# A two-layer graph-attention kernel: query numbers of 16 groups by GpSimd gathers, W2's loads begun by ScalarE and its stores by SyncE

## The chip, the cores and the metric

The kernel runs on one core of one Trainium2 chip. The metric is the device time of one execution in microseconds (us), as the median of several runs. Engines: TensorE (PE; its weight loads are PEld), VectorE (DVE), ScalarE (ACT), GpSimd (POOL), SyncE (SP). SyncE, ScalarE and GpSimd can begin DMA transfers, each from its own in-order queue of instructions; "SPq", "ACTq" and "POOLq" in a profile are such beginnings.

## What is computed

Two layers of relational graph attention over 3125 nodes of 768 features and 53125 edges sorted by destination, with three relations; then a residual and a layer norm. One layer, cut to what matters:

```python
xr = jnp.einsum('nd,rdf->rnf', x, W)          # a row per node and relation
oi, oj = xr[etype, dst], xr[etype, src]
alpha = leaky_relu(oi @ q + oj @ k, 0.2)      # per edge and head: 4 heads, then 1
e = jnp.exp(alpha - segment_max(alpha, dst)[dst])
a = e / (segment_sum(e, dst)[dst] + 1e-16)
out = segment_sum(a * oj, dst) + b            # then elu after the first layer
```

An edge's query number `oi @ q` depends on its destination and relation alone, so per node there are 3 relations x 4 heads = 12 of them in the first layer.

## The kernel before

The nodes are cut into 25 groups of up to 128. A group's edges lie in 17 slots of 128 (14 in group 0), one edge per partition. There are three stages. The first multiplies every node by the three W1 matrices and stores the rows in a table in DRAM (`tab1`, named ftab in the profile). The second gathers a row for each edge, slot by slot, with GpSimd's indirect DMAs (`gather_rows`, L468), and sums them by destination on TensorE; it also makes the table for the second layer, of which the third stage gathers. Products of 32-bit numbers are three TensorE products of high and low parts each. The scores of the second stage read the query numbers from `pall`, one for each slot, edge and head, which the first stage fills.

The first stage is one written-out order. Each turn of `phase1`'s loop (L787 on) issues what the table `ev` holds for it, then one piece of the dense products: 18 matmuls 386 or 398 columns wide into one of two result banks (`banks`, po in the profile). A group has 6 pieces. ScalarE copies the result into one of six half rows (`d_row`, L581), which frees the bank, and SyncE stores it (L583). Every engine runs its own instructions in that order and waits only for the data and buffers that an instruction needs. The turn at which a step is issued is `when(turn, step, ...)`.

In the same loop a group's query numbers reach its edges. The last piece of a group also holds the 12 query numbers per node. VectorE splits them into three bf16 parts (`split3`, L207 to L212) and SyncE stores them in `q1_d`. Later SyncE loads the group's destinations over all partitions (`s_load1`, 544 KB, tile sT, L530) and the nodes' query numbers (`q_load1`, tile q, L540); VectorE turns the destinations into a 0/1 matrix (`a_q`, L680) and the relations into another (`a_oh`, L686); TensorE multiplies (`a_q2`, 17 matmuls of 36 columns, results pq); VectorE picks by relation and adds (`a_q3`, L708 and L711) into `pall`.

The second layer's W2 is prepared there too, in 18 pieces of 128 rows: `w_load` begins a load from GpSimd's queue (L745; two transfers for a piece of the last two of six), `w_split` two turns later casts on ScalarE (L752) and subtracts on VectorE (L753) into the single tile w2hl, and takes two weighted sums (L756). Of the first 12 pieces both parts are stored in DRAM (`w2_d`): by SyncE for the first four, by GpSimd for the rest (L759), and read back late in the stage (`second_weights`). GpSimd has nothing else in the loop besides these transfers.

Of the kernel before, what the change touches and what calls it, by code (L numbers as in the profile page):

```python
# [9 lines left out]
F32 = mybir.dt.float32  # L10
# [3 lines left out]
I32 = mybir.dt.int32  # L14
AF = mybir.ActivationFunctionType
ALU = mybir.AluOpType
# [5 lines left out]
P = 128  # L22
# [4 lines left out]
BIG = float(2**100)  # L27
# [35 lines left out]
def _index(ap):  # L63
    return bass.IndirectOffsetOnAxis(ap=ap, axis=0)
# [3 lines left out]
SL = 17  # L68
# [13 lines left out]
WHOLE = 2  # L82
# [27 lines left out]
def kernel(  # L110
# [21 lines left out]
    nc = tc.nc  # L132
    N, D = x.shape
    R = layers[0]["W"].shape[0]
    E = src.shape[0]
    NB = (N + P - 1) // P
    NP = NB * P
    DT = D // P
    HALF = D // 2
    l1, l2 = layers  # L140
    H1 = l1["H"]
# [5 lines left out]
    HW = RW // 2  # L147
    EARLY = 6
    GB = NB - 4
# [4 lines left out]
    V, S, G, T = nc.vector, nc.scalar, nc.gpsimd, Counted(nc.tensor)  # L154
    OOB = float(1 << 20)

    dram = ctx.enter_context(tc.tile_pool(name="fdram", bufs=1, space=DRAM))
# [6 lines left out]
    tab2 = dram.tile([NP * R, RW], F32, name="ftab2")  # L164
    xb_d = dram.tile([NP + P, D], F32, name="xb_d")
    q1_d = dram.tile([NP + P, H1 * R * 3], BF, name="q1_d")
    w2_d = dram.tile([R * DT * P, 2 * D], F32, name="w2_d")

    ident = keep.tile([P, P], F32, name="fident")
# [26 lines left out]
    pall = keep.tile([P, NB, SL, H1], F32, name="pall")  # L196
# [7 lines left out]
    def split3(to, q, work, shape):  # L204

        c = work.tile(shape, F32, name="c3", bufs=2)
        V.tensor_copy(to[0], q)  # L207
        V.tensor_sub(c, q, to[0])
        V.tensor_copy(to[1], c)
        c2 = work.tile(shape, F32, name="c3", bufs=2)  # L210
        V.tensor_sub(c2, c, to[1])
        V.tensor_copy(to[2], c2)  # L212
# [242 lines left out]
    def slots(b):  # L455
        return SL if b else SLF
# [85 lines left out]
    def feature_rows(t):  # L542

        if t < H1:
            return [(0, t * F1, P)]
        o = P - (F1 - P)
        return [(0, (2 * (t - H1)) * F1 + P, F1 - P), (o, (2 * (t - H1) + 1) * F1 + P, F1 - P)]
# [31 lines left out]
    def d_row(o, q, b, p, po):  # L579

        S.copy(o[:, :HW], po[:, :HW])  # L581
        to = tab1[b * P * R:(b + 1) * P * R, :].rearrange("(p r) f -> p r f", r=R)
        nc.sync.dma_start(to[:, p // 2, p % 2 * HW:(p % 2 + 1) * HW], o[:, :HW])  # L583
        if p == len(PIECES1) - 1:
            q1s = q.tile([P, H1 * R, 3], BF, name="q1s", bufs=2)
            split3([q1s[:, :, i] for i in range(3)], po[:, HW:HW + H1 * R], q, [P, H1 * R])
            nc.sync.dma_start(q1_d[b * P:(b + 1) * P, :], q1s.rearrange("p k s -> p (k s)"))

    def stretches(rows, at_, a, e):

        i = a
        while i < e:
            c = at_(i) % len(rows)
            k, c = rows[c]
            n = 1
            while i + n < e and rows[at_(i + n) % len(rows)][0] is k and rows[at_(i + n) % len(rows)][1] == c + n:
                n += 1
            yield i, i + n, k[:, c:c + n, :]
            i += n

    def phase1(pre, work, psum, left, due, more):
        st = a_st
# [13 lines left out]
        def a_index2(b):  # L616
            pT = st[b]["pi"]
            c = SL
            V.tensor_scalar(dl[:, b, :], pT[:, c:2 * c], 1.0 / BIG, n_all[:, b:b + 1], op0=ALU.mult,
                            op1=ALU.subtract)  # L620
            inv = work.tile([P, SL], F32, name="inv", bufs=2)
            V.tensor_scalar(inv, dl[:, b, :], float(P), OOB, op0=ALU.is_ge, op1=ALU.mult)
            V.tensor_add(ridx[:, b, :], pT[:, 0:SL], inv)
            if b in first_rows:
                V.tensor_scalar(rfirst[:, first_rows[b], :], ridx[:, b, :], NP * R - 1, None, op0=ALU.min)
            V.tensor_copy(rel[:, b, :], pT[:, 2 * c:3 * c])

        counts = work.tile([32, 32], F32, name="counts", bufs=1)
        V.memset(counts, 0.0)
# [52 lines left out]

        def a_oh(b):
            s = st[b]
            s["oh"] = work.tile([P, SL, R * 3], F32, name="oh", bufs=2)
            V.tensor_tensor(s["oh"], rel[:, b, :, None].to_broadcast([P, SL, R * 3]),  # L686
                            rel3.rearrange("p r s -> p (r s)")[:, None, :].to_broadcast([P, SL, R * 3]),
                            op=ALU.is_equal)
# [46 lines left out]
        w2 = {}  # L735
        kq2 = work.tile([P, 2, D], F32, name="kq2", bufs=1)

        def w_load(i):
            if i == 0:
                for s, name in ((0, "k"), (1, "q")):  # L740
                    nc.sync.dma_start(kq2[:, s, :], l2[name].rearrange("f h -> h f").to_broadcast([P, D]))
            r, t = divmod(i, DT)
            w2[i] = share[3][:, :D]
            for p, at, n in feature_rows(t):
                G.dma_start(w2[i][p:p + n], l2["W"][r, at:at + n, :])  # L745

        def w_split(i):
            w = w2.pop(i)
            r, t = divmod(i, DT)
            if r < WHOLE:  # L750
                hl = work.tile([P, 2, D], F32R, name="w2hl", bufs=1)
                S.copy(hl[:, 0, :], w)  # L752
                V.tensor_sub(hl[:, 1, :], w, hl[:, 0, :].bitcast(F32))  # L753
            for s in range(2):
                j = work.tile([P, D], BF, name="w2j", bufs=1)
                V.scalar_tensor_tensor(j, w, 1.0, kq2[:, s, :], op0=ALU.mult, op1=ALU.mult,  # L756
                                       accum_out=wkq2[:, t, (Q2 if s else K2)[r]:][:, 0:1])
            if r < WHOLE:
                (G if i >= 4 else nc.sync).dma_start(w2_d[i * P:(i + 1) * P, :].rearrange("p (s f) -> p s f", s=2), hl.bitcast(F32))  # L759

        def pad_rows():

# [7 lines left out]
        def when(n, f, *a):  # L770
            ev.setdefault(n, []).append((f, a))

        TAIL = 6 * (GB - 1)
        S0 = 10
        when(8, pad_rows)
        for b in range(NB):
            c = S0 + 5 * b
            when(c - 3 if b else S0 - 1, c_load, work, b)
            when(c - 2 if b else S0 - 1, a_load, pre, b)
            when(c + 1, a_index, b)  # L780
            when(c + 2, a_index2, b)
            when(c + 1, c_next, b)
            q = max(c + 1, 6 * b + 2)
            if b < GB:
                k = (q, q, q, q + 3, q + 3, q + 4, q + 5)
            else:
                q = max(c + 2, 6 * GB + 4 + 2 * (b - GB))  # L787
                e = 6 * NB - 5 + b - GB
                k = (q, 6 * NB - 14 + b - GB, 6 * NB - 5, q + 5, e, e, e)
            for n, f in zip(k, (s_load1, q_at, q_load1, a_q, a_oh, a_q2, a_q3)):  # L790
                when(n, f, b)
            if b > 1:
                t, e = {2: (2, 4), 3: (3, 10), GB: (TAIL - 8, TAIL - 3), GB + 1: (TAIL - 7, TAIL), GB + 2: (TAIL - 6, TAIL - 2), GB + 3: (TAIL - 5, TAIL - 1)}.get(
                    b, (6 * b - 11, 6 * b - 8))
                when(t, d_load, b)
                when(e, d_split, b)
            when(5 * b + 2, p_load, b)
            when(5 * b + 5, p_plus, b)
        when(S0 + 5 * NB, a_last)
        for i in range(R * DT):  # L800
            when(6 * (2 + i), w_load, i)
            when(6 * (2 + i) + 2, w_split, i)
        for p, (r, f, n) in enumerate(((0, 0, HW), (0, HW, D - HW), (1, 0, HW), (1, HW, D - HW))):
            when(TAIL + 4 * p + 5, second_weights, r, f, n)
        for c in range(2):
            when(TAIL + 10 + 8 * c, second_kq, c)
        for n in range(2, max(max(ev), 6 * NB) + 1):
            if n < 10:
                more(2)
            for f, a in ev.get(n, ()):  # L810
                f(*a)
            next(left, None)
            while len(due) > (n < 6 * NB - EARLY - 1):
                d_row(outs[len(outs_used) % len(outs)], work, *due.pop(0))
                outs_used.append(0)
# [715 lines left out]
    with tc.manual_schedule():  # L1531
        with tc.tile_pool(name="share", bufs=1) as pool:
# [5 lines left out]
            with tc.tile_pool(name="wbuf", bufs=1) as wbuf:  # L1538
                weights[0] = [wbuf.tile([P, DT, WA], F32R, name=f"wa{s}") for s in "HL"]
                with tc.tile_pool(name="wrest", bufs=1) as wrest, tc.tile_pool(name="pre", bufs=1) as pre:  # L1540
# [16 lines left out]
                    with tc.tile_pool(name="work0", bufs=1) as work, tc.tile_pool(  # L1557
                        name="psum0", bufs=1, space=PSUM
# [22 lines left out]
                    with tc.tile_pool(name="work1", bufs=1) as work, tc.tile_pool(  # L1581
                        name="psum1", bufs=1, space=PSUM
                    ) as psum:
                        pools.append(psum)
                        phase1(pre, work, psum, left, due, more)
                with tc.tile_pool(name="exbuf", bufs=1) as exbuf:
                    extra = exbuf.tile([P, NX, RW], F32, name="extra")
                    with tc.tile_pool(name="work2", bufs=1) as work, tc.tile_pool(
                        name="psum2", bufs=1, space=PSUM
                    ) as psum:  # L1590
                        phase2(work, psum)
                    with tc.tile_pool(name="work3", bufs=1) as work, tc.tile_pool(
                        name="psum3", bufs=1, space=PSUM
# [545 lines left out]
```

## Time and profile before

| | us |
|---|---|
| runs | 1765.5, 1759.7, 1765.43; median 1765.43 |
| profiled execution | 1765.7 |
| its span | 1763.9 |
| last dense product of the first stage starts at | 530.5 |
| first row gather of the second stage starts at | 534.3 |
| first matmul of the second stage starts at | 551.4 |

| engine | busy us of the span | instructions |
|---|---|---|
| TensorE | 1648.9 (93%) | 14093 |
| VectorE | 1116.9 (63%) | 3911 |
| ScalarE | 438.0 (25%) | 805 |
| GpSimd | 901.3 (51%) | 907 |

In rows of groups, "x16 | 12.8, 538 | 188.5 <-DVE" means 16 instructions, 12.8 us busy, 538 ns each in the mean, and 188.5 us in which the engine stood idle just before them, with what ended it. In a timeline a row gives start, duration, engine, line, operation, what is written from what, and in brackets the idle time before it. In a table by stretch, each engine has its busy time and its count of instructions, then come TensorE's granted clock, the mean busy share of the 16 DMA engines, and GB/s. In a list of waits stand the total, the number and the longest.

### The profile page before, as it was taken

The numbers are of one execution on the slowest core, as the hardware profiler recorded it, in microseconds if no ns is written. First come the engines' busy times: TensorE is split into PE (matmuls) and PEld (weight loads), VectorE is DVE, ScalarE is ACT, GpSimd is POOL, SyncE is SP. The second block draws the span as 40 slices with busy tenths as digits, with TensorE's granted clock in tenths as the row PEclk, the third lists the DMA queues.
The fourth block names the chain that finished last, engine by engine and source line by source line (L and its number), as shares of the span: only waits on it lengthen the run. The fifth ranks groups of instructions, "written<-read, shape, count | busy, mean of one in ns | idle before, by whom it ended". The sixth has DMA issues, their size and how long they took to land. (4 is left out here: it accounts for less than half of the span.)

```text
span 1763.9 us, 38699 instructions
## 1 busy us (share of the span) xinstructions
PE 1648.9 (93%) x14093; PEld 1282.5 (73%) x14093; DVE 1116.9 (63%) x3911; ACT 438.0 (25%) x805; POOL 901.3 (51%) x907
## 2 busy tenths in 40 slices
PE   8999999999993899999999999939999999999996
PEld 8999999999992688888888888825444444444443
DVE  7566667566525666666677777455666666666663
ACT  6222222211210122121221112212333333333331
POOL 4100000000006777777777777057777777777760
PEclk9999999999996899999999999969999999999998
DMA  8576766656577999999999999469999999999970
GB/s 271 177 243 218 217 224 231 199 171 209 187 266 266 322 350 359 354 349 348 347 345 347 342 349 343 131 218 317 340 339 335 341 336 334 337 337 341 340 274 20
DMA packets 169367, 501.55 MB, mean 284 GB/s; under 512 B 39890, under 2 KB 82489, under 8 KB 169166
## 3 DMA queue, kind: packets, MB, share of 16 engines
q0 software_dynamic: 70832, 343.91, 55.1%
q1 hardware_dynamic: 90104, 144.97, 24.8%
q10 hardware_dynamic: 8230, 10.10, 1.7%
q8 instruction: 113, 1.85, 0.4%
q14 instruction: 88, 0.72, 0.1%
HBM read 414.04 MB, written 89.63 MB: 286 GB/s over the span
## 5 line engine op out<-in xcount | busy, mean ns | idle before, releaser
L468 POOL DMA_INDIRECT extra<-ftab,ridx x296 | 301.6, 1019 | 94.4 <-issue 52.7
L53 PE MATMUL po<-waH,hT 128*128 128x386 f32 (+1 forms) x1200 | 326.2, 346 | 1.4 <-DVE hT L1031 0.7
L53 PE MATMUL po<-waH,xT 128*128 128x386 f32 x1104 | 294.6, 343 | 0.9 <-ACT xT L255 0.4
L468 POOL DMA_INDIRECT share<-ftab,ridx x209 | 211.5, 1012 | 68.9 <-issue 41.0
L53 PEld LDWEIGHTS po<-waH,hT 128*128 128x128 f32 x1200 | 216.6, 189 | 4.8 <-DVE hT L1031 1.1
L53 PE MATMUL D<-extra,AT 128*128 128x256 f32 (+1 forms) x600 | 211.4, 504 | 5.3 <-ACT AT L1399 5.3
L53 PEld LDWEIGHTS po<-waH,xT 128*128 128x128 f32 x1104 | 203.9, 190 | 1.4 <-DVE xT L256 0.8
L53 PE MATMUL po<-waL,hT 128*128 128x386 f32 (+1 forms) x600 | 203.0, 338 | 0.0
L53 PE MATMUL po<-waL,xT 128*128 128x386 f32 x552 | 188.3, 341 | 3.1 <-DVE wbH L416 3.0
L53 PEld LDWEIGHTS D<-extra,AT 128*128 128x128 f32 x600 | 113.9, 196 | 69.6 <-issue 48.3
L581 ACT COPY share<-po 128x386 f32<-128x386 f32 x150 | 72.3, 482 | 368.9 <-PE po L53 296.4
L53 PE MATMUL acc<-waL,marks 128*32 128x386 f32 (+1 forms) x860 | 151.9, 489 | 0.0
L53 PE MATMUL po<-wbH,xT 128*128 128x386 f32 (+1 forms) x552 | 147.5, 341 | 0.9 <-DVE g L410 0.9
L53 PE MATMUL acc<-waH,marks 128*32 128x384 f32 (+1 forms) x828 | 140.4, 493 | 0.7 <-DVE marks L1321 0.7
L53 PE MATMUL acc<-extra,marks 128*32 128x386 f32 (+1 forms) x564 | 129.5, 487 | 0.0
L468 POOL DMA_INDIRECT waL<-ftab,ridx x108 | 107.9, 999 | 33.6 <-issue 25.3
L53 PE MATMUL acc<-extra,sel 128*32 128x193 f32 x2736 | 122.9, 332 | 2.3 <-DVE sel L940 2.3
L468 POOL DMA_INDIRECT waH<-ftab,ridx x103 | 103.7, 1007 | 31.4 <-issue 25.3
L53 PEld LDWEIGHTS po<-waL,hT 128*128 128x128 f32 x600 | 113.3, 189 | 0.0
L53 PE MATMUL acc<-share,marks 128*32 128x384 f32 (+1 forms) x456 | 109.7, 487 | 0.0
L745 POOL DMA_DIRECT2D share<-in_L_gnn_W_dram x24 | 12.8, 538 | 188.5 <-DVE w2j L756 117.1
L53 PEld LDWEIGHTS acc<-extra,sel 128*32 128x32 f32 x2736 | 86.5, 111 | 30.4 <-issue 4.9
(286 smaller groups left out, 2990.9 us busy)
## 6 DMA issues: line engine op xcount, KB each, us to landing
ftab<-share SPq DMA_DIRECT2D x150, 193.0 KB
ftab<-r SPq DMA_DIRECT2D x50, 386.0 KB
sT<-dr_d SPq DMA_DIRECT2D x23, 544.0 KB
xb_d<-share SPq DMA_DIRECT2D x25, 384.0 KB
ftab<-y SPq DMA_DIRECT2D x100, 96.0 KB
share<-xb_d SPq DMA_DIRECT2D x25, 384.0 KB
share<-in_x_dram SPq DMA_DIRECT2D x24, 384.0 KB
out_dram<-share SPq DMA_DIRECT2D x24, 384.0 KB
```

Of the source, the lines that this page charges most:

```text
L53: return self.add(self.engine.matmul(to, weights, moving, **more), to, moving)
L468: return G.indirect_dma_start(out=to, out_offset=None, in_=tab, in_offset=_index(i[:, j:j + 1]), bounds_check=NP * R - 1, oob_is_err=False)
L581: S.copy(o[:, :HW], po[:, :HW])
L745: G.dma_start(w2[i][p:p + n], l2["W"][r, at:at + n, :])
```

## The change

`by_gather(b)` is true for groups 0 to 18 without 4, 9 and 14: 16 groups of 25. For these the steps `s_load1`, `q_at`, `q_load1`, `a_q`, `a_oh`, `a_q2` and `a_q3` are not issued any more. Instead every group's 12 query numbers per node are also copied as they are (`q1f`) and stored in a new table `q1r_d` with a row of four for each node and relation; `a_index2` makes the row number of each edge (`qi`), and `q_gather` has GpSimd gather a slot's rows straight into `pall`: 128 rows of 16 bytes, 269 times. `pall` is zeroed first, as rows out of bounds are not written. The tile `oh` has one buffer instead of two. All of W2's loads begin on ScalarE, and the stores of its first 12 pieces on SyncE, in a step of their own two turns after the split.

```diff
+    q1r_d = dram.tile([NP * R, H1], F32, name="q1r_d")
@@ d_row, a group's last piece
             nc.sync.dma_start(q1_d[b * P:(b + 1) * P, :], q1s.rearrange("p k s -> p (k s)"))
+            q1f = q.tile([P, R, H1], F32, name="q1f", bufs=2)
+            V.tensor_copy(q1f, po[:, HW:HW + H1 * R].rearrange("p (h r) -> p r h", h=H1))
+            nc.sync.dma_start(q1r_d[b * P * R:(b + 1) * P * R, :].rearrange("(p r) h -> p r h", r=R), q1f)
@@ a_index2
+            if by_gather(b):
+                d = work.tile([P, SL], F32, name="qd", bufs=2)
+                V.scalar_tensor_tensor(d, pT[:, c:2 * c], R / BIG, pT[:, 2 * c:3 * c], op0=ALU.mult, op1=ALU.add)
+                st[b]["qi"] = work.tile([P, SL], I32, name="qi", bufs=7)
+                V.tensor_add(st[b]["qi"], d, inv)
+        def by_gather(b):
+            return b < GB - 1 and b % 5 != 4
+        def q_gather(b, j):
+            n = (b + 1) * P * R
+            G.indirect_dma_start(out=pall[:, b, j, :], out_offset=None, in_=q1r_d[:n, :],
+                                 in_offset=_index(st[b]["qi"][:, j:j + 1]), bounds_check=n - 1, oob_is_err=False)
@@ a_oh
-            s["oh"] = work.tile([P, SL, R * 3], F32, name="oh", bufs=2)
+            s["oh"] = work.tile([P, SL, R * 3], F32, name="oh", bufs=1)
@@ w_load
-                G.dma_start(w2[i][p:p + n], l2["W"][r, at:at + n, :])
+                nc.scalar.dma_start(w2[i][p:p + n], l2["W"][r, at:at + n, :])
@@ w_split, w_store
-                (G if i >= 4 else nc.sync).dma_start(w2_d[i * P:(i + 1) * P, :].rearrange("p (s f) -> p s f", s=2), hl.bitcast(F32))
+                w2hl[i] = hl
+        def w_store(i):
+            nc.sync.dma_start(w2_d[i * P:(i + 1) * P, :].rearrange("p (s f) -> p s f", s=2), w2hl.pop(i).bitcast(F32))
@@ the table of turns
+        when(8, G.memset, pall, 0.0)
-            for n, f in zip(k, (s_load1, q_at, q_load1, a_q, a_oh, a_q2, a_q3)):
-                when(n, f, b)
+            if by_gather(b):
+                for j in range(slots(b)):
+                    when(max(6 * b + 9, c + 3) + j * 7 // SL, q_gather, b, j)
+            else:
+                for n, f in zip(k, (s_load1, q_at, q_load1, a_q, a_oh, a_q2, a_q3)):
+                    when(n, f, b)
             when(6 * (2 + i) + 2, w_split, i)
+            if i < WHOLE * DT:
+                when(6 * (2 + i) + 4, w_store, i)
```

On GpSimd, from the last transfers of the edge preparation on, the order before was this, with `share` the tile that W2's pieces are loaded into and `w_d` the table for its parts:

```order
L299 DMA share<-ed_d 125x553
L279 DMA ed_d<-e 125x425
L279 DMA dr_d<-share 125x425
L279 DMA ed_d<-e 125x425
L745 DMA share<-in_L_gnn_W_dram 128x768 x4
L745 DMA share<-in_L_gnn_W_dram 64x768 x2
L759 DMA w_d<-w2hl 128x1536
L745 DMA share<-in_L_gnn_W_dram 64x768 x2
L759 DMA w_d<-w2hl 128x1536
```

From the same place the order now is this, up to the second stage's first row gathers (ftab_62 is `tab1`):

```order
L300 DMA share<-ed_d 125x553
L280 DMA ed_d<-e 125x425
L280 DMA dr_d<-share 125x425
L280 DMA ed_d<-e 125x425
L842 MEMSET pall 128x1700
L644 DMA pall<-q1r_d,qi 128x4 x269
L469 DMA share<-ftab_62,rfirst 128x772 x9
```

W2's transfers have left GpSimd's queue, and the zeroing and 269 query gathers stand ahead of the row gathers.

On ScalarE, in the early loop of the first stage, the copies that free the result banks (po) stood before between the casts of x (xT) and of W2 (w2hl):

```order
L581 COPY share<-po_778 128x386
L581 COPY share<-po_777 128x386
L752 CAST w2hl<-share 128x768
L581 COPY share<-po_778 128x386
L581 COPY share<-po_777 128x386
L255 CAST xT<-xr 128x768
```

The same piece of a group now:

```order
L582 COPY share<-po_779 128x386
L582 COPY share<-po_778 128x386
L764 DMA share<-in_L_gnn_W_dram 128x768
L582 COPY share<-po_779 128x386
L582 COPY share<-po_778 128x386
L771 CAST w2hl<-share 128x768
L582 COPY share<-po_779 128x386
L582 COPY share<-po_778 128x386
L256 CAST xT<-xr 128x768
```

The load of a W2 piece stands in ScalarE's own queue now, two copies ahead of the cast that needs it.

More of the change, by code (lines that the diff above doesn't have):

```diff
@@ L758, in w_split @@
             if r < WHOLE:
-                (G if i >= 4 else nc.sync).dma_start(w2_d[i * P:(i + 1) * P, :].rearrange("p (s f) -> p s f", s=2), hl.bitcast(F32))
+                w2hl[i] = hl
+        w2hl = {}
+        def w_store(i):
+            nc.sync.dma_start(w2_d[i * P:(i + 1) * P, :].rearrange("p (s f) -> p s f", s=2), w2hl.pop(i).bitcast(F32))
         def pad_rows():
```

## The prediction

> **What bounds the kernel now.** I read the span first, then a table of busy time by stretch over the first stage, then who waited for whom on TensorE there, then the timelines of five engines where that stage ends.
>
> ```profile
> span 1763.9 us, 38699 instructions
> ...
> core 0: us, PE busy (x) PEld busy (x) DVE busy (x) ACT busy (x) POOL busy (x), PEclk, DMA share, GB/s
> ...
> 194.00:213.00 19.00, 19.00 (x123) 18.84 (x122) 14.07 (x59) 4.36 (x8) 1.12 (x2) 1.00 0.79 250
> ...
> 498.00:517.00 19.00, 19.00 (x109) 19.00 (x108) 2.49 (x6) 2.90 (x6) 0.00 (x0) 1.00 0.97 358
> ...
> PE po L53 <- DVE wbH L416: 3.0, 1, 3.0
> ```
>
> In the two stretches TensorE is busy for all of their 19 us at full clock, with VectorE, ScalarE and GpSimd partly or almost wholly idle. The last row is TensorE's longest wait between 45 and 530 us, 3.0 us in the weight preparation, before the groups' loop; the others add little over 1 us and lie there too. So the first stage lasts as long as TensorE's own list of matmuls.
>
> ```profile
> 530.49 0.34 PE L53 MATMUL po<-wbH,xT 128*128 128x398 f32 x1
> ...
> 530.91 0.48 ACT L581 COPY share<-po 128x386 f32<-128x386 f32 x1 [2.78 <-PE po L53]
> ...
> 531.41 0.32 SPq L583 DMA_DIRECT2D ftab<-share  x1
> ...
> 531.42 0.18 DVE L207 CAST q1s<-po 128x12 bf16<-128x12 f32 x1 [2.24 <-ACT share L581]
> ...
> 532.26 0.18 DVE L212 CAST q1s<-c 128x12 bf16<-128x12 f32 x1
> ...
> 534.34 1.12 POOL L468 DMA_INDIRECT share<-ftab,rfirst  x1 [113.32 <-DMA q_d<-q1s]
> ...
> 544.92 1.00 POOL L468 DMA_INDIRECT share<-ftab,rfirst  x1 [0.30 <-issue]
> ...
> 548.83 1.00 POOL L468 DMA_INDIRECT extra<-ftab,rfirst  x1 [0.30 <-issue]
> ...
> 550.73 0.22 DVE L881 TENSOR_TENSOR a<-pall,share 128x36 f32<-128x36 f32 x1 [3.90 <-issue]
> ...
> 551.39 0.80 PE L56 MATMUL pa<-fident,al 128*32 128x128 f32 x3 [10.28 <-DVE al L883]
> ```
>
> Read it as a chain: last table product, its copy, its store (VectorE splits the query numbers meanwhile), then GpSimd's first row gather of the second stage, then eight more of them before VectorE's first add. It hangs on the last product. GpSimd had been idle for 113 us before, so whatever ends the products earlier moves the whole second stage earlier, as long as GpSimd is free by then.
>
> **The change, part by part.** TensorE first: 16 of the 25 groups lose their 17 query matmuls, 272 in all.
>
> ```profile
> 107.48 0.34 PE L53 MATMUL po<-waH,xT 128*128 128x386 f32 x1
> 107.66 0.59 PE L53 MATMUL pq<-q,sT 128*128 128x36 bf16 x17
> 108.10 0.42 PE L53 MATMUL po<-waH,xT 128*128 128x386 f32 x1
> 108.36 0.34 PE L53 MATMUL po<-waL,xT 128*128 128x386 f32 x1
> ...
> 203.66 0.48 ACT L581 COPY share<-po 128x386 f32<-128x386 f32 x1 [1.96 <-PE po L53]
> 206.85 0.48 ACT L581 COPY share<-po 128x386 f32<-128x386 f32 x1 [2.71 <-PE po L53]
> ...
> 210.55 0.48 ACT L581 COPY share<-po 128x386 f32<-128x386 f32 x1 [2.48 <-issue]
> ```
>
> From the product before the block to the second product after it pass 108.36 - 107.48 = 0.88 us; two products alone take 2 x 3.19/18 = 0.35 us (3.19 = 206.85 - 203.66, a turn of 18 products). The block costs 0.53 us. ScalarE's copies give 3.70 - 3.19 = 0.51. I take 0.53, which is read on the engine itself: 16 x 0.53 = 8.5 us (8.2 by the other), all of it on the path.
>
> GpSimd gets 269 gathers of four numbers per partition (14 for group 0, 17 for 15 more). None of that kind is in the trace; the nearest have the same 128 indices and longer rows.
>
> ```profile
> L468 POOL DMA_INDIRECT extra<-ftab,ridx x224 | 229.7, 1025 | 72.4 <-issue 36.0 <-PE po L53 13.1 <-PE acc L53 11.2
> ...
> 551.00:1110.00 559.00, 539.19 (x6404) 460.53 (x6408) 386.24 (x1092) 106.69 (x232) 417.65 (x410) 0.98 0.96 340
> ...
> 571.00 1.37 POOL L468 DMA_INDIRECT share<-ftab,rfirst  x1 [0.30 <-DVE F L898]
> ...
> 92.94 1.71 DVE L613 STREAM_TRANSPOSE pi<-T 32x32 f32<-32x32 f32 x8 [1.98 <-DMA T<-ed_d]
> ```
>
> Lower end: 1.02 us each with no gap, 274 us. Upper end: every one as slow as 1.37 and 0.30 between, 1.67 us each, 449 us. I take the mean of 1.02 and the 0.30 gap: 1.32 us each, 355 us. The first may start near 95 us, once group 0's indices are turned (92.94 + 1.71), and GpSimd must be free at 534.34 - 8.5 = 525.8. That leaves 431 us for 269 gathers, 1.60 us each. So 1.32 is hidden with some 75 us to spare, spread over the stage as the groups come; 1.67 would end at 544, 18 us late. What makes 1.32 the nearer end is that 224 gathers average 1.02 in a stage in which VectorE is busy for 386 of 559 us, as much as in the first.
>
> The gathers' bytes, and what goes:
>
> ```profile
> 532.00:533.00 1.00, 0.00 (x0) 0.00 (x0) 0.59 (x4) 0.00 (x0) 0.00 (x0) 1.00 0.52 198
> 533.00:534.00 1.00, 0.00 (x0) 0.00 (x0) 0.00 (x0) 0.00 (x0) 0.00 (x0) 0.65 0.09 9
> ...
> 540.00:545.00 5.00, 0.67 (x17) 0.59 (x17) 4.62 (x11) 0.00 (x0) 3.78 (x5) 0.50 0.95 333
> ```
>
> In the second row all that moves is one store of query numbers, 128 pieces of 72 bytes: 0.09 us of the 16 DMA engines. A gather of 128 pieces of 16 bytes is nearest to that: 269 x 0.09 = 24 us over 430. The first row is one 193 KB store in 0.52 us, so the 16 broadcasts of 544 KB that go free 16 x 1.5 = 23 us. The two cancel. The other end is a gather of whole table rows (third row: 0.95 of 5 us for about 3.8 of them, 1.24 us each): 334 us, and the DMA engines would be full. Those carry 386 KB against 2 KB, so I do not take it.
>
> ScalarE gets 24 W2 load issues and, in its queue, what stands behind them: the copies that free TensorE's two result banks, and the cast of W2 (L752), which now waits for a load issued only two copies earlier.
>
> ```profile
> 183.71 0.42 SPq L250 DMA_DIRECT2D xr<-in_x_t_dram  x1
> ...
> 189.65 0.83 ACT L255 CAST xT<-xr 128x768 fp32r<-128x768 f32 x1 [1.99 <-DMA xr<-in_x_t_dram]
> ...
> 194.05 0.48 ACT L581 COPY share<-po 128x386 f32<-128x386 f32 x1 [3.19 <-PE po L53]
> ...
> 200.49 0.48 ACT L581 COPY share<-po 128x386 f32<-128x386 f32 x1 [2.71 <-PE po L53]
> 200.87 0.83 ACT L752 CAST w2hl<-share 128x768 fp32r<-128x768 f32 x1
> ```
>
> The load would be issued after the copy at 194.05, near 194.5, and is wanted at 200.9: 6.4 us. The slowest load of that size that ScalarE waited for in the loop took 183.71 to 189.65, 5.9 us. If it is late, the next copy, which would start at 203.66, may wait until its bank is wanted a turn later, at 206.8: it must start by 206.3, the 0.83 us cast before it by 205.4, and 10.9 us are allowed. I cost it at nothing. The bounds are nothing and, were every load 1 us later than that, 12 casts x 1 = 12 us. An issue like the first row's takes 0.42 us, against idle gaps of 2.7.
>
> SyncE loses 16 broadcasts and 16 query loads with their address reads, and gets 25 small stores and 8 more stores of W2's halves. It issues a row store within 0.5 us of its copy (530.91 to 531.41), and six half-row buffers stand behind that, so one issue of 0.32 us more or less costs nothing; a W2 store waits for a split of two turns before and has four turns, 12.8 us, until the next cast takes its tile. VectorE loses an equality, an outer test, two products and a sum for each of 16 groups; it gets two operations on 17 numbers for each, and 25 copies of 12 numbers from a result bank. Those copies hold the bank of a group's last piece longer, after five conversions (531.42 to 532.44, the product over at 530.83): released 1.8 us after the product, needed after 3.2. Cost nothing; 25 x 0.18 = 5 us if no slack were there. GpSimd's zeroing of the query numbers comes once, in its empty stretch before 95 us. One buffer less for the test's tile changes nothing, since VectorE writes and reads both in order.
>
> The sum is 1765.7 (the profiled execution, 1.8 over its span) - 8.5 = **1757.2 us**. The median of the runs shown, 1765.43, is the same to 0.3; one run of the three was 1759.7. A difference under 0.5% (8.8 us) is about what a measurement of this kernel cannot tell from no change, and the sum stands just inside it.
>
> **The rivals.** *GpSimd becomes the bound of the first stage* (slower). Place: its last query gather against its first row gather. It decides from 1.60 us a gather on. VectorE's long operations could hold GpSimd up:
>
> ```profile
> L756 DVE SCALAR_TENSOR_TENSOR w2j<-share,kq 128x768 bf16<-128x768 f32 x36 | 34.4, 955 | 1.8 <-DMA kq<-in_L_gnn_q_dram 0.9 <-DMA kq<-in_L_gnn_k_dram 0.3
> L732 DVE TENSOR_TENSOR share<-share 128x768 f32<-128x768 f32 x25 | 23.7, 950 | 17.0 <-DMA share<-in_x_dram 16.9
> ...
> L680 DVE TENSOR_SCALAR sT<-sT,cols 128x2176 bf16<-128x2176 bf16 x23 | 17.8, 776 | 1.0 <-DMA sT<-dr_d 1.0
> ...
> L753 DVE TENSOR_TENSOR w2hl<-share,w2hl 128x768 fp32r<-128x768 f32 x12 | 11.5, 956 | 10.8 <-ACT w2hl L752 10.8
> L256 DVE TENSOR_TENSOR xT<-share,xT 128x768 fp32r<-128x768 f32 x11 | 10.5, 954 | 14.2 <-ACT xT L255 14.2
> L256 DVE TENSOR_TENSOR xT<-xr,xT 128x768 fp32r<-128x768 f32 x10 | 9.6, 957 | 16.0 <-ACT xT L255 16.0
> ```
>
> These are 107.5 of 470 us (60 to 530), 23%. If GpSimd stood still in all of them, a gather would take 1.32/0.77 = 1.71 us, the last would end at 95 + 460 = 555, 29 us after 525.8, and the time would be 1757 + 29 = 1786. Against it: in the second stage VectorE is busier still and gathers take 1.02 against 1.00 with it idle (548.83). But the operations there are other ones, so I leave 9%.
>
> The Trainium skill has a rule for this: "SBUF — State Buffer", section "SBUF: two separate sides", says that VectorE and GpSimd share one pair of ports as an exclusive lock, taken by VectorE's fast modes and its operations on two SBUF inputs, and that DMA descriptors written by GpSimd starve meanwhile. By that rule the time is this rival's, 1786; the second stage's 1.02 us does not bear out a large loss, and no row of before shows a gather beside the operations listed.
>
> *The queues give the gain back* (about no change). ScalarE stands behind a W2 load or behind a transfer slot, the copies come late, TensorE waits for a bank: 12 casts x 0.7 us would return 8.4 us, time 1766. That needs loads of 10.9 + 0.7 = 11.6 us on average; for it speaks that ScalarE did wait for a load once it was 5.9 us old, against it that none was near 10. 11%.
>
> *The DMA engines fill up* because the small pieces cost like table rows: over 430 us they would carry the loop's own 0.79 x 430 = 340 us, less 23, and 334 more, 221 us too much: 1978. The bytes speak against it. 2%.
>
> **How the numbers follow.** Forecast 78%, with a range of its own of 1752 to 1761 (2 us for a side cost, 5.7 for the spread of the runs, mostly below). GpSimd 9%, queues 11%, DMA 2%. The range 1751 to 1769 takes in the forecast's and most of the queues' case and leaves out the 11% of the slower ones and a few per cent below. Faster by over 0.5% is below 1756.6: half of the forecast's case, 38%. Slower is GpSimd and DMA, 11%. The rest, 51%, is the same.
>
> **What would show it.** Right: 153 query matmuls, the last product near 522 us instead of 530.5, GpSimd's gathers at about 1.3 us and done before 470, the first row gather near 526, later stages as long as before. Wrong: TensorE waiting for ScalarE's copy near a W2 cast; query gathers still running when the last table store has landed; a DMA share near 1 all through the stage. It would also be wrong low if the stage's turns were shortened by more than the matmuls taken out, for which no row speaks.

## The result, and the profile after

The changed kernel took 1757.4 us (median of 16 runs, 1753.6 to 1762.0), the kernel before 1763.4 us beside it (16 runs, 1758.1 to 1768.2): ratio 0.9969, 95% interval 0.9957 to 0.9982, a gain of 5.5 us (3.2 to 7.6); the two medians lie 6.0 apart. The forecast was 1757.2, from a gain of 8.5. The median lies 0.2 us from it only because the three runs of before that it started from stood 2 us above the 16; the gain is the number to explain, and it was forecast too large.

The page of the profiled execution (1756.9 us), its span, the row of the new gathers (busy us and mean ns of one, then the idle time before them), and the answer for TensorE's query products (pq):

```profile
span 1755.2 us, 38591 instructions
...
L644 POOL DMA_INDIRECT pall<-q1r_d,qi x269 | 290.4, 1079 | 95.7 <-issue 77.7
...
L53 PE MATMUL pq<-q,sT x119: 177/178/211, 171.5 to 531.6; 128*128 128x36 bf16 x119
...
L53 PE MATMUL pq<-q,share x17: 190/194/195, 528.3 to 528.8; 128*128 128x36 bf16 x17
...
L53 PE MATMUL pq<-q,xr x12: 194/195/213, 531.9 to 532.3; 128*128 128x36 bf16 x12
...
L53 PE MATMUL pq<-q,w2j x5: 195/195/195, 532.3 to 532.4; 128*128 128x36 bf16 x5
...
L644 POOL DMA_INDIRECT pall<-q1r_d,qi x269: 992/997/1812, 97.4 to 468.4; - x135
```

These are 153 query products, as forecast. The same answer for before has 391, 17, 12 and 5; 272 are gone, as many as the 16 groups had. The last row is the gathers' shortest, median and longest time in ns, and when the first and the last started. One stretch of the loop, in the columns of the prediction's table, shows who got the work, TensorE as full as before and GpSimd busy for 15 of 19 us:

```profile
194.00:213.00 19.00, 19.00 (x109) 19.00 (x108) 10.06 (x40) 4.36 (x8) 15.03 (x14) 1.00 0.70 200
```

The end of the first stage, which answers to the prediction's second set of rows:

```profile
523.07 0.34 PE L53 MATMUL po<-wbH,xT 128*128 128x398 f32 x1
...
523.49 0.48 ACT L582 COPY share<-po 128x386 f32<-128x386 f32 x1 [2.78 <-PE po L53]
...
525.48 0.38 SPq L591 DMA_DIRECT2D q1r_d<-q1f  x1
526.82 1.00 POOL L469 DMA_INDIRECT share<-ftab,rfirst  x1 [57.40 <-DMA q1r_d<-q1f]
...
542.72 0.22 DVE L912 TENSOR_TENSOR a<-pall,share 128x36 f32<-128x36 f32 x1 [4.02 <-DMA share<-ftab,rfirst]
543.38 0.80 PE L56 MATMUL pa<-fident,al 128*32 128x128 f32 x3 [10.74 <-DMA extra<-ftab,rfirst]
```

The chain is as it was: last product, copy, first row gather 3.75 us after the product (3.85 before), nine gathers, second stage. It starts 7.4 us earlier, and GpSimd had been idle for 57.4 us when it was wanted. From the second stage's first matmul to the end of the span the two executions take the same, 1212.5 us before and 1211.8 after.

To tell the loop from the rest, two rows of ScalarE do: its 21st copy out of a result bank, just after the first group's query products in before, and its 150th, the last of the stage. Before, and then after:

```profile
107.90 0.48 ACT L581 COPY share<-po 128x386 f32<-128x386 f32 x1 [2.71 <-PE po L53]
```

```profile
107.91 0.48 ACT L582 COPY share<-po 128x386 f32<-128x386 f32 x1 [2.72 <-DMA ftab<-share]
```

With the last copies at 530.91 (a row of the prediction) and 523.49 the loop between takes 423.01 us before and 415.58 after: 7.43 less. Copy by copy, the difference grows by 0.45 to 0.53 us at each of the 16 groups and falls twice, by 0.70 at the copy near 182 us and by 0.47 near 453. At both places TensorE now waits for VectorE (waits of TensorE from 45 to 530 us; in before neither is there):

```profile
PE po L53 <- DVE fdl L623: 0.4, 1, 0.4
...
PE po L53 <- DVE q1f L590: 0.2, 1, 0.2
```

At both, TensorE goes on 0.15 us after the end of q1f's copy out of the bank; `fdl` is the operation of VectorE behind that copy.

### The profile page after: what moved, and what is told of

It reads as the page before. It is cut to its first block, busy times and chain, and to the rows that moved or that the text cites. A ratio compares the mean times of both kernels' runs of the same rounds, so it can differ in the third digit from the quotient of the medians.

```text
span 1755.2 us, 38591 instructions
## 1 busy us (share of the span) xinstructions
PE 1640.4 (93%) x13821; PEld 1274.8 (73%) x13821; DVE 1086.4 (62%) x3888; ACT 437.8 (25%) x805; POOL 1177.4 (67%) x1145
## 5 line engine op out<-in xcount | busy, mean ns | idle before, releaser
L644 POOL DMA_INDIRECT pall<-q1r_d,qi x269 | 290.4, 1079 | 95.7 <-issue 77.7
```

The source lines that it names most:

```text
L644: G.indirect_dma_start(out=pall[:, b, j, :], out_offset=None, in_=q1r_d[:n, :], in_offset=_index(st[b]["qi"][:, j:j + 1]), bounds_check=n ...
```

## The experiments

They ran on two kinds of chip. On one the kernel before takes 1762 to 1763 us; on the other, where eight of the twelve ran (four on each of two chips), 2001 to 2002 us. Each ratio is to the kernel before on the same chip. The table has the loop (21st to last copy) of each profiled execution, which can be compared across chips as long as TensorE alone sets it.

| kernel | before there, us | time, us | ratio (95%) | loop, us |
|---|---|---|---|---|
| before | 1763 | 1763.4 | | 423.0 |
| changed | 1763 | 1757.4 | 0.9969 (0.9957 to 0.9982) | 415.6 |
| r1, changed again | 1762 | 1757.8 | 0.9976 (0.9963 to 0.9989) | 415.6 |
| r2, gathers only | 1762 | 1805.9 | 1.0243 (1.0213 to 1.0274) | 460.3 |
| r3, bank copy first | 1762 | 1756.9 | 0.9971 (0.9957 to 0.9986) | 414.5 |
| e6, 18 groups, bank copy first | 1762 | 1758.2 | 0.9969 (0.9954 to 0.9985) | 413.4 |
| e1, queues only | 2001 | 2014.3 | 1.0068 (1.005 to 1.0085) | 423.1 |
| e3, without the gathers | 2001 | 2007.3 | 1.0026 (1.001 to 1.0042) | 415.5 |
| e2, gathers only | 2001 | 2172.8 | 1.0851 (1.0824 to 1.0877) | 584.4 |
| e4, bank copy first | 2001 | 2204.1 | 1.1037 (1.1002 to 1.1071) | 597.3 |
| e5, 20 groups | 2002 | 2237.9 | 1.1188 (1.1142 to 1.1235) | 635.7 |
| e10, W2's stores back | 2002 | 2182.4 | 1.0914 (1.0874 to 1.0954) | 582.4 |
| e8, two-input operations | 2002 | 2164.5 (one run) | | 564.9 |
| e9, one-input operations | 2002 | 2192.8 (one run) | | 594.7 |

**Queues only (e1).** `by_gather` is false for all groups; the new table, its copies and the zeroing are out.

```diff
-            return b < GB - 1 and b % 5 != 4
+            return False
```

> Only the queues are changed: W2's loads begin on ScalarE and its stores on SyncE; no group's query numbers are gathered, and the new table, its copies and the zeroing are not there. Theory (the gain is TensorE's lost query matmuls alone, the queues are worth nothing): 425 query matmuls stand again, the last dense product starts near 530.5 us, and the time is that of the kernel before, ratio 0.999 to 1.001. Rival A (the queues cost part of the gain, which is why 5.5 us were measured and not 8.5): 1 to 3 us slower than before, with TensorE waiting for ScalarE's copies near the loads. Rival B (the queues themselves bring the gain): 3 us or more faster.

The loop's first and last copy:

```profile
109.25 0.48 ACT L581 COPY share<-po 128x386 f32<-128x386 f32 x1 [2.71 <-PE po L53]
...
532.35 0.48 ACT L581 COPY share<-po 128x386 f32<-128x386 f32 x1 [2.78 <-PE po L53]
```

The loop is 423.1 us, that of before on the other chip to 0.1: in the first stage the move of the queues neither costs nor brings anything by itself. The whole time is 13.7 us over before's on that chip, against all three expectations. There is no trace of before from that chip, and where these lie stays open.

**Without the gathers (e3).**

```diff
-                    when(max(6 * b + 9, c + 3) + j * 7 // SL, q_gather, b, j)
+                    pass
```

> The changed kernel with the 269 query gathers left out, so that 16 groups' query numbers stay zero; indices, the new table, its copies and the queues stay. Theory (the gathers are hidden wholly): time as the changed kernel's, ratio to before 0.996 to 0.998, last product near 523.1 us. Rival (the gathers disturb VectorE or the transfers of the first stage, and that is the missing 1 to 3 us): 1 to 3 us faster than the changed kernel, last product at 520.5 to 522.3 us.

```profile
111.54 0.48 ACT L582 COPY share<-po 128x386 f32<-128x386 f32 x1 [2.72 <-PE po L53]
...
527.05 0.48 ACT L582 COPY share<-po 128x386 f32<-128x386 f32 x1 [2.78 <-PE po L53]
```

The loop is 415.5 us against 415.6 with them on the other chip, and TensorE has the same two new waits (0.4 and 0.2): the gathers cost TensorE nothing on the faster chip, so the microsecond between 8.5 and 7.4 is not theirs. Against e1 on the same chip the loop is 7.6 us shorter and the median 7.0 us.

**Bank copy first (e4, then r3 where before takes 1762 us).**

```diff
+            q1f = q.tile([P, R, H1], F32, name="q1f", bufs=2)
+            V.tensor_copy(q1f, po[:, HW:HW + H1 * R].rearrange("p (h r) -> p r h", h=H1))
             split3([q1s[:, :, i] for i in range(3)], po[:, HW:HW + H1 * R], q, [P, H1 * R])
...
-            q1f = q.tile([P, R, H1], F32, name="q1f", bufs=2)
-            V.tensor_copy(q1f, po[:, HW:HW + H1 * R].rearrange("p (h r) -> p r h", h=H1))
```

> The changed kernel with VectorE's copy of the query numbers out of the result bank (q1f) moved ahead of the five conversions of the split. Theory (part of the missing microsecond is TensorE waiting for that bank, 0.41 us at 449 us and 0.2 to 0.4 us near 179 us): the waits of TensorE on q1f go, what is left is behind ScalarE's copies and the split, the last product starts 0.3 to 0.9 us earlier than 523.1 us, and the time is 0.3 to 0.9 us lower, too little for the ratio to tell. Rival (the bank is held by the split anyway, whichever comes first): the same total of waits, now on the split's last operation, last product unchanged.

> The changed kernel with the copy q1f ahead of the split, once more. Where the kernel before takes about 1763 us: by theory the waits of TensorE on q1f go and the last product starts 0.3 to 0.9 us earlier than the changed kernel's 523.1; by the rival (the split holds the bank anyway) it stays within 0.2 us, with the same waits under another name; if the edit itself were what cost 10% on the other chip, it is at 1.10 here too. Where it takes about 2000 us: as the changed kernel beside it, to 1%.

r3's 21st and last copies:

```profile
105.20 0.48 ACT L582 COPY share<-po 128x386 f32<-128x386 f32 x1 [2.71 <-DMA ftab<-share]
...
519.71 0.48 ACT L582 COPY share<-po 128x386 f32<-128x386 f32 x1 [2.78 <-PE po L53]
```

Loop 414.51 us, 8.50 less than before: 16 x 0.53 = 8.5, the forecast's sum. Both of TensorE's new waits are gone, and with them 1.07 us. That is the term that the prediction had put at nothing. The ratio, as expected, can't tell it.

**The changed kernel again (r1).**

> The changed kernel once more, as it is. On the chip of the first four experiments the kernel before took 2001 us, not 1763, two kernels without gathers stood at 1.003 and 1.007 of it, and two with gathers at 1.085 and 1.104. Theory 1 (that chip, not the edits of those two kernels, makes the gathers dear): where the kernel before takes about 2000 us, the changed kernel is 8 to 10% slower too, ScalarE's copies start up to 20 us late while gathers run, and the last dense product starts near 720 us; where the kernel before takes about 1763 us, ratio 0.996 to 0.998 and 523 us. Theory 2 (those edits themselves cost that): the changed kernel is at 0.996 to 0.998 on either chip.

Ratio 0.9976 and a loop of 415.60 us, 0.02 from the first trace. Here r1 and r3 agree to 0.1% while on the other chip e4, the same file as r3, was 10% slower: the chip makes that, not the edit. That the changed kernel itself is slower there was not run; six kernels with its gathers were, and took 8 to 12% more than before.

**Gathers only (e2, then r2).** W2's loads and stores stand where they were before.

```diff
-                nc.scalar.dma_start(w2[i][p:p + n], l2["W"][r, at:at + n, :])
+                G.dma_start(w2[i][p:p + n], l2["W"][r, at:at + n, :])
...
-                w2hl[i] = hl
+                (G if i >= 4 else nc.sync).dma_start(w2_d[i * P:(i + 1) * P, :].rearrange("p (s f) -> p s f", s=2), hl.bitcast(F32))
...
-            if i < WHOLE * DT:
-                when(6 * (2 + i) + 4, w_store, i)
```

> Only the gathers are added: W2's loads and stores stand in the queues they had before, so that on GpSimd they stand behind query gathers. Theory (the move of the queues is a condition of the gain): a group's 17 gathers take 17 x 1.38 = 23.5 us against 19.15 us of a group's turns, so GpSimd falls up to some 14 us behind the order before a group without gathers lets it catch up; a W2 load then begins up to 14 us late where 5 us of slack were reckoned (10.9 allowed, 5.9 for the load), ScalarE's cast and the copies behind it are late, and TensorE waits some 9 us in all, perhaps 20: ratio to before 1.000 to 1.008, last product at 531 to 543 us. Rival (GpSimd's queue has room enough for both): as the whole change, ratio 0.996 to 0.998, last product near 523 us.

> The kernel with the gathers alone once more: W2's loads and stores stand in the queues they had before. Where the kernel before takes about 1763 us: by the theory that the move of the queues is a condition of the gain, GpSimd is up to 14 us behind its order when a W2 load stands in it, casts and copies come late, ratio 1.000 to 1.008, last product at 531 to 543 us; by the rival (GpSimd's queue has room for both) ratio 0.996 to 0.998, last product near 523 us. Where it takes about 2000 us: ratio near 1.085 as before.

ScalarE's waits for W2's loads from 90 to 575 us in r2 (total, number, longest), the beginning of a W2 load on GpSimd, and the cast that waited for it:

```profile
ACT w2hl L771 <- DMA share<-in_L_gnn_W_dram: 64.3, 9, 11.5
```

```profile
178.35 0.59 POOL L764 DMA_DIRECT2D share<-in_L_gnn_W_dram  x1
```

```profile
169.85 0.48 ACT L582 COPY share<-po 128x386 f32<-128x386 f32 x1 [2.71 <-PE po L53]
181.81 0.83 ACT L771 CAST w2hl<-share 128x768 fp32r<-128x768 f32 x1 [11.48 <-DMA share<-in_L_gnn_W_dram]
182.55 0.86 ACT L582 COPY share<-po 128x386 f32<-128x386 f32 x2
```

The load begins only after the gathers ahead of it, at 178.35; the cast, whose turn had come at 170.3, waits 11.5 us, and two copies behind it, starting at 182.55, run one right after the other, too late for TensorE. In the changed kernel no cast of W2 waits for its load. The direction was expected, the size not: 44.8 us more than the changed kernel's loop, against 9 to 20. Nine casts are late, not one. TensorE's waits of this stretch add up to 30.0 us, 26.6 of them for ScalarE's copies. The other 15 go with a lower granted clock, the third number from the end in r2's row for 109 to 200 us:

```profile
109.00:200.00 91.00, 77.05 (x426) 75.61 (x426) 45.98 (x189) 16.65 (x31) 66.29 (x64) 0.92 0.57 163
```

It is 0.95 to 0.97 from 200 to 500 us; the changed kernel has 1.00 in all of these. What lowers it is not shown.

**18 groups (e6).** With the bank copy first, as in r3.

```diff
-            return b < GB - 1 and b % 5 != 4
+            return b < GB - 1 and b % 10 != 9
```

> The changed kernel with 18 groups gathered instead of 16 (303 gathers; all but 9 of groups 0 to 18) and q1f ahead of the split. Theory (each group more takes 0.53 us from TensorE as long as GpSimd is done in time): at 1.38 us each the gathers end at 97 + 303 x 1.38 = 515 us, ahead of the 525 us at which the first row gather may start; last product near 521.5 us, time 1 to 2 us under the changed kernel's, ratio 0.995 to 0.997. Rival (GpSimd falls behind its order, since groups without a gather are what lets it catch up, and the last groups' gathers come after 525): first row gather up to 10 us later, ratio 1.000 to 1.004. Where the kernel before takes about 2000 us: worse than the changed kernel beside it, ratio over 1.10.

Its gathers, and its first row gather:

```profile
L644 POOL DMA_INDIRECT pall<-q1r_d,qi x303: 992/997/1778, 100.9 to 518.3; - x152
```

```profile
528.11 0.99 POOL L469 DMA_INDIRECT share<-ftab,rfirst  x1 [8.85 <-DMA q_d<-q1s]
```

Two groups more take 1.08 us more from the loop (413.43), against 2 x 0.53; 303 gathers take 417 us, 1.38 each, and end 8.85 us before GpSimd is wanted. This is about as many as fit, since another group's 17 take 23. The loop is the shortest of all, but the median is not below r3's or the changed kernel's. (The profiled execution, the slowest of its seven, reached its 21st copy at 111.39 us, 6.2 later than r3's; that tells nothing of the median.) A version measurably better than the changed kernel was not found.

**20 groups (e5) and W2's stores back (e10).**

```diff
-            return b < GB - 1 and b % 5 != 4
+            return b < GB - 1
```

```diff
-                w2hl[i] = hl
+                (G if i >= 4 else nc.sync).dma_start(w2_d[i * P:(i + 1) * P, :].rearrange("p (s f) -> p s f", s=2), hl.bitcast(F32))
...
-            if i < WHOLE * DT:
-                when(6 * (2 + i) + 4, w_store, i)
```

> The changed kernel with 20 groups gathered (0 to 19, 337 gathers) instead of 16. Theory (GpSimd becomes the bound when its gathers do not fit between 96 and 525 us, at 1.38 us each 310 of them): they end at 96 + 337 x 1.38 = 561 us; the last dense product comes 4 x 0.53 = 2.1 us earlier than the changed kernel's, the first row gather waits for GpSimd's own queue until 561 instead of 526, and the time is some 34 us over the changed kernel's: ratio to before 1.015 to 1.020. Rival (GpSimd keeps up, since its gathers shorten when VectorE has less to do for these groups): the gathers end before 525, ratio 0.994 to 0.997.

> The changed kernel with W2's stores back where they were, behind the split and for pieces 4 to 11 on GpSimd; its loads stay on ScalarE. Theory (only the loads had to leave GpSimd, since a cast waits for them): the stores stand behind gathers, their tile comes free late, but no load does; GpSimd waits some 10 to 20 us in all for the splits, its gathers end near 480 to 490 us, well before 525, and time and last product are the changed kernel's within 1 us, ratio 0.996 to 0.998. Rival (the stores cost too: the single tile w2hl is held until GpSimd has stored it, so the next cast on ScalarE and the copies behind it are late): TensorE waits for ScalarE's copies, 5 to 20 us, ratio 1.000 to 1.009.

Both ran on the slower chip, where the loop waits for something else, and neither answers its question: in e5 GpSimd stood idle for 69 us before its first row gather, so it was not the bound, and e10 lies between e2 and e4. Beyond 303 gathers the limit is untried, and so is which of loads and stores had to move.

What the slower chip does shows in e4's waits from 45 to 700 us, of TensorE, then of ScalarE, and in one of ScalarE's copies:

```profile
PE po L53 <- issue: 99.2, 17, 25.4
PE po L53 <- ACT share L582: 40.2, 7, 12.0
```

```profile
ACT share L582 <- remote: 232.4, 24, 29.0
```

```profile
168.66 0.48 ACT L582 COPY share<-po 128x386 f32<-128x386 f32 x1 [17.36 <-remote]
```

The product that this copy takes was done by 154.2, and the store that frees its half row, six copies earlier, was begun at 135.07, but it starts at 168.66, 2.3 us after the last of eleven gathers that ran meanwhile. Without gathers (e1, e3) the loop has none of this. What holds the copies there is not settled: "remote" says that the trace has no releaser, and no run tells the possible ones apart.

**Operations beside the gathers (e8, e9).** One more operation of VectorE in each of 90 turns, nothing reads its result.

```diff
+        def extra_op():
+            j = work.tile([P, D], BF, name="w2j", bufs=1)
+            V.tensor_tensor(j, kq2[:, 0, :], kq2[:, 1, :], op=ALU.add)   # e8
+            V.tensor_copy(j, kq2[:, 0, :])                               # e9, instead
...
+        for n in range(20, 110):
+            when(n, extra_op)
```

> The changed kernel with one more operation of VectorE in each of 90 turns of the first stage, 768 numbers per partition from two SBUF inputs (a sum of kq2's two halves into the scratch tile w2j, which nothing reads). In the changed kernel 47 of 269 gathers took over 1.1 us and lie beside such operations. Theory (VectorE's operations on two SBUF inputs hold GpSimd's gathers up): about as many more are stretched by about half a microsecond, the gathers' busy sum goes from 290 to 305 to 330 us and the last starts 15 to 40 us later than 468 us. Rival (it is a chance of the order; the gathers are stretched by something else): sum 288 to 293 us, end as before. By both TensorE's last product stays within 2 us.

> As the kernel beside it, but the operation added in each of 90 turns is a copy of 768 numbers per partition from one SBUF input. Theory (two SBUF inputs are what holds a gather up): the gathers' busy sum stays at 288 to 295 us and their end at 468 us to 5 us. Rival (any long operation of VectorE on SBUF does): the sum goes to 305 us or more, as with two inputs.

Both on a slower chip. Groups of e8, then of e9:

```profile
L644 POOL DMA_INDIRECT pall<-q1r_d,qi x269 | 304.0, 1130 | 187.7 <-issue 77.7 <-DVE qi L635 74.8 <-DMA q1r_d<-q1f 19.5
...
L787 DVE TENSOR_TENSOR w2j<-kq 128x768 bf16<-128x768 f32 x90 | 85.7, 952 | 0.8
```

```profile
L644 POOL DMA_INDIRECT pall<-q1r_d,qi x269 | 281.4, 1046 | 245.9 <-DVE qi L635 98.4 <-issue 77.4 <-DMA q1r_d<-q1f 32.4
...
L787 DVE CAST w2j<-kq 128x768 bf16<-128x768 f32 x90 | 51.3, 570 | 0.8
```

In e4, on another of the slower chips, with the bank copy first and without either operation, the sum is 279.8 us: 24 less than with the operations on two inputs, 2 less than with those on one. Read by the sums, two inputs would be what counts, as expected. The single gathers say otherwise. A copy of e9, and a gather that begins inside it:

```profile
361.97 0.56 DVE L787 CAST w2j<-kq 128x768 bf16<-128x768 f32 x1
```

```profile
362.10 1.30 POOL L644 DMA_INDIRECT pall<-q1r_d,qi  x1 [0.30 <-issue]
```

It finds 0.43 us of the copy left and takes 0.30 longer than 1.00. In e9, 29 gathers begin inside an added copy, and those with 0.16 to 0.43 us of it left take 0.03 to 0.30 longer: the rest less 0.13, which is also what an operation on two inputs costs. In e8, 38 begin inside an added sum and take 0.47 longer in the mean, 17.7 us in all. The copies cost only 2.0 in all because they are shorter (0.55 us against 0.95) and 11 of the 29 gathers meet one in its last 0.06 us. So one input from SBUF holds a gather up too, and the theory of e9 is wrong, though the sum hardly moved. When the gathers end can't be compared, since the loop itself is stretched.

## Why the prediction was right, and where not

**What bounds the kernel** and the chain at the stage's end were right: what came off the loop moved the second stage by as much or a little more (product 7.4 earlier, row gather 7.5, first matmul of the second stage 8.0).

**TensorE's 16 x 0.53 us** was right in the sum to 0.02 us: r3's 8.50 shows it, and e6 that two groups more give 2 x 0.54.

**"Cost nothing" for q1f's copy out of the bank** was the step that failed. It reckoned 1.8 us of holding against 3.2 of slack, from a place where VectorE came at once. At two places VectorE came late: near 178 us behind small operations of the edge preparation, near 448 behind one of 1.03 us and one of 0.95. The first of them, with TensorE's next product into that bank (the one before it had ended at 175.42):

```profile
178.00 0.17 DVE L209 TENSOR_TENSOR c<-po,q1s 128x12 f32<-128x12 f32 x1
...
178.71 0.16 DVE L590 COPY q1f<-po 128x12 f32<-128x12 f32 x1
```

```profile
179.02 0.41 PE L53 MATMUL po<-waH,xT 128*128 128x386 f32 x1 [0.40 <-DVE fdl L623]
```

Only the first two of the split's five conversions read the bank, the second of them at 178.00. So without q1f the bank is free 2.7 us after its product; with q1f behind all five it is held for 3.45 us, and for 3.80 at the other place. That cost 1.1 us, near the lower of the two ends given (0 and 5). r3 shows it by taking it away.

**From 7.4 to 5.5 us** (4.2, with 1.9 to 6.5, in r1) the rest is not shown. Most of both intervals lies below 7.4, so something outside the loop seems to take 2 to 3 us back. The two profiled executions do not show it: their spans differ by 8.7 us. Two things vary there between executions of one kernel: the start (21st copy at 107.91 and 106.01 in two traces of the changed kernel) and the granted clock, which in the loop of both kernels is 1.00. Over the runs of r1 and of before beside it the clock's mean was 0.9733 for before (22 runs) and 0.9721 for the changed kernel (10 runs); (1 - clock) x time is 47 and 49 us, 2 us of it. Among runs of equal clock (0.972, 0.973, 0.974) r1's lie 6.1, 5.8 and 6.3 us below before's, with 2 to 6 runs each. So the clock goes with a part of the difference; whether the change lowers it, and how, is not shown. Nor is it excluded that the move of the queues costs something outside the loop: e1's 13.7 us on the slower chip lie there.

**GpSimd's gathers.** Forecast 1.32 us each and done before 470; the pitch was 371.1/268 = 1.38, the last began at 468.4. They were hidden, with 57 us to spare. The 0.06 comes from 47 gathers of over 1.1 us, and they show how the rival (GpSimd becomes the bound) went wrong. VectorE and GpSimd of the changed kernel, in one place:

```profile
185.84 0.96 DVE L751 TENSOR_TENSOR share<-share 128x768 f32<-128x768 f32 x1 [3.11 <-DMA share<-in_x_dram]
187.65 0.96 DVE L257 TENSOR_TENSOR xT<-xr,xT 128x768 fp32r<-128x768 f32 x1 [0.85 <-ACT xT L256]
```

```profile
185.20 0.99 POOL L644 DMA_INDIRECT pall<-q1r_d,qi  x1 [0.30 <-issue]
186.50 1.17 POOL L644 DMA_INDIRECT pall<-q1r_d,qi  x1 [0.30 <-issue]
187.98 1.50 POOL L644 DMA_INDIRECT pall<-q1r_d,qi  x1 [0.32 <-issue]
```

The operation at 185.84 begins inside a gather, which stays at 0.99. The gather at 186.50 begins inside it, with 0.30 us of it left, and takes 0.17 longer; that at 187.98 finds 0.63 left of the next and takes 0.50 longer. So it is nearly everywhere: 51 gathers begin inside such an operation on two inputs and take 0.41 us longer in the mean, nearly always the operation's rest less 0.13; the 40 in which one begins are not lengthened, and of the other 178 only three are (1.11, 1.37 and 1.81 us; the second begins inside an operation on sT, with one input). 51 x 0.41 = 21 us is nearly the whole of what 290.4 has over 269 x 1.00. The rival let GpSimd stand still in all of VectorE's 107 us of long operations; the gathers lost a fifth of that, since an operation that finds a gather under way doesn't stop it.

The Trainium skill, "SBUF — State Buffer", section "SBUF: two separate sides", says that VectorE and GpSimd contend for one pair of ports, VectorE when it is in a fast mode or has two SBUF inputs (then only against a GpSimd instruction that reads SBUF), and that whichever starts first has the pair for its whole instruction while the other fully blocks. Where VectorE starts first the trace agrees, but for the 0.13 us. Where the gather starts first it does not: VectorE's operations beside gathers stay at 0.94 to 0.98 us, so the block is seen on GpSimd alone. The prediction read the rule as stopping GpSimd in all of these operations, and so left out the gathers that start first; of starved descriptors that section speaks for fast modes alone. e9's copies hold a gather up as a fast mode would, but no view names an operation's mode.

**Queues.** The rival that they give the gain back was wrong for the loads as moved: no cast waited. Leaving them costs 45 us (r2), which the prediction did not price.

**DMA engines.** Their share over the loop (the last number but one) did not rise by more than 0.01, as the two terms that cancel would have it. Before, and then after:

```profile
108.00:523.00 415.00, 415.00 (x2631) 411.73 (x2627) 254.57 (x937) 84.60 (x159) 16.16 (x30) 1.00 0.67 218
```

```profile
108.00:523.00 415.00, 414.38 (x2406) 412.96 (x2405) 225.18 (x917) 85.61 (x161) 281.85 (x262) 1.00 0.68 201
```

## What to carry to other kernels

Price matmuls that leave a bound TensorE by the spacing of their neighbours: 0.53 us a block held to 0.02. Then look for what the change adds behind TensorE's result banks: a short copy added behind five conversions, of which only the first two read the bank, cost an eighth of the gain, and nothing when it was moved to the front. Before an engine's in-order queue is filled with small work, take out of it every transfer that another engine waits for: the same gathers made the kernel 0.3% faster with W2's loads and stores moved and 2.4% slower without. And where a sum over many instructions answers a question, look at single ones too: the sums of e8 and e9 seemed to set one input apart from two, and the gathers inside their operations did not.

## What the runs showed of the hardware that was not expected

A gather on GpSimd that begins during a 0.96 us operation of VectorE on two SBUF inputs is held nearly to its end, and one already under way is not touched (1.41 against 1.00 us in the mean). A copy or scalar operation with one input, from SBUF to SBUF, does the same (0.43 us left of a cast, 1.30; 0.50 left of one on sT, 1.37). Operations that read a result bank do not (0.30 left of `tq`, 1.00), and neither does the sum over `tq` behind them (0.46 left in r1, 1.00).

On a chip where the kernel before takes 2001 us instead of 1763, the first stage without gathers runs at the same pace (loop 423.1 and 415.5 us), while the part from the second stage's first matmul on takes 1437 us (e1 to e4) instead of 1212 and 269 small gathers stretch the loop by 150 to 180 us (564.9 to 597.3 in e8, e10, e2, e9 and e4). A gain of 0.3% that rests on GpSimd's gathers is a gain on one of these chips only, as far as the kernels run here show.
